# Lower halves of 18 of h's 49 tiles: by diagonal matmuls on TensorE and a copy on ScalarE instead of one instruction on VectorE

## The chip, the cores and the metric

The kernel runs on one core of a Trainium2 chip, as one launch. The metric is the device time of that launch in microseconds. Before the change it was 1441.87 us, the median of three runs (1438.64 to 1441.97).

## The reference, cut to what matters

A layer of a graph network: 6250 nodes with 256 values each, 200,000 edges sorted by target, a mixture of 64 experts with the best two for each node, a batch norm, and a layer norm at the end. What bears on the change is its first part:

```python
deg_out = jnp.clip(segment_sum(ones, src, num_segments=n), 1.0)
h = feats * jax.lax.rsqrt(deg_out)[:, None]
m = segment_sum(h[src], dst, num_segments=n) * jax.lax.rsqrt(deg_in)[:, None]
gc = m @ W_gc + b_gc
x = gc + (feats @ W_res + b_res)
```

The kernel multiplies by W_gc first, so its rows of h are feats @ W_gc times the factor rsqrt(deg_out) of their node, which it calls s_out.

## The kernel before, in words

The nodes are held in 49 tiles of 128 rows (NS = 49, the last tile with 106). A first stage, up to about 155 us, finds the degrees by matmuls of one-hots and projects the nodes (`project`). What it projects lands unscaled in `hrow[:, u, D:2D]`, by a DMA from the tile `hx` (line 623).

Then each row is scaled and split in two numbers, so that TensorE's faster float32r format keeps its accuracy: `upper(t)` (line 404, ScalarE) writes the product with s_out, rounded to float32r, into `hrow[:, u, :D]`, and `lower(t)` (line 409, VectorE) puts what the rounding left, product minus upper half, in the place of the unscaled values. Both work on two tiles a call, t - 1 and t, with t odd; `halves(t)` calls the two. After every four or six tiles `lower` writes these rows to `h_dram` (line 192, on SyncE's queue).

The stage that uses h is `dense()`. It is a generator of pieces of work; the loop at line 1176 runs them in the order in which they are yielded, and puts in pieces of another kind (`gather`) by their estimated durations. Inside `tc.manual_schedule()` each engine's instructions stand in this written order, and each engine works through its own in order; only semaphores tie them together. `dense()` runs windows c of edges:

- `lo_of` and `hot_of` (lines 386 and 837, VectorE) make tables of one-hots, `count(g)` (line 859, TensorE) multiplies two of them into a bank `pc` of PSUM, ScalarE casts the bank to `room` (line 871, 876 or 879), and VectorE adds its first column (line 902, `carried`).
- `multiply(c, t)` (lines 914 and 915, TensorE) multiplies the counts of window c by the lower and the upper half of tile t. The counts of window c + 1 are made between the multiplies of window c.
- In the opening (40 counts of window 0) a call of `halves` follows each four counts, which make one bank. From there, as long as tiles are left, one follows every second multiply of window 0, with about three counts between two calls.

The rows of h that went to DRAM come back in `gather`: GpSimd fetches 128 of them at a time by index (line 768), TensorE multiplies them (lines 773 and 774). The first fetch waits until all of h is written. The stage of the experts and the norms begins at about 880 us and isn't touched.

PSUM is cut into pools. The pool `ps_g` has one bank, in which `gather` adds up, as the tile `pg`.

Of the kernel before, what the change touches and what calls it, by code (L numbers as in the profile page):

```python
# [9 lines left out]
F32 = mybir.dt.float32  # L10
F32R = mybir.dt.float32r
# [4 lines left out]
AF = mybir.ActivationFunctionType  # L16
# [13 lines left out]
NS = -(-N // SP)  # L30
ODD = N - (NS - 1) * SP
D = 256
# [8 lines left out]
WIN = 128  # L41
# [8 lines left out]
FIRSTS = 32  # L50
PAIRS = 8
MARGIN = 48


SIZES = ((1, 416), (2, 400), (3, 368), (5, 352), (7, 320), (10, 288), (12, 272), (17, 256), (21, 240), (25, 224), (31, 208), (34, 192), (40, 176), (45, 160), (46, 144), (50, 128), (63, 112), (64, 80))
# [119 lines left out]
def gnn_moe_kernel(ctx, tc, x_in, x_cols, src, dst, bases, nexts, firsts, parts, lasts, W_gc, b_gc, W_res, b_res, Wg, bg, w1, b1, w2, b2,  # L175
                   gamma, beta, out):
    nc = tc.nc
    V, S, G, T = nc.vector, nc.scalar, nc.gpsimd, nc.tensor
# [9 lines left out]
    def source_out(tile_ap, ap, t0, n):  # L188

        whole = min(n, NS - 1 - t0)  # L190
        if whole > 0:
            nc.sync.dma_start(out=ap[t0 * SP:(t0 + whole) * SP, :].rearrange("(t p) d -> p t d", p=SP),
                              in_=tile_ap[:, :whole, :])
        if t0 + n >= NS:
            for a, b in ((0, 96), (96, ODD)):
                nc.sync.dma_start(out=ap[(NS - 1) * SP + a:(NS - 1) * SP + b, :], in_=tile_ap[a:b, NS - 1 - t0, :])
# [24 lines left out]
    def f32(ap):  # L221
        return ap.bitcast(F32)
# [128 lines left out]
    with tc.tile_pool(name="edges", bufs=1) as ep, ExitStack() as later:  # L351
# [50 lines left out]
        def upper(t):  # L402
            for u in range(t - 1, min(t + 1, NS)):
                S.activation(hrow[:, u, :D], f32(hrow[:, u, D:2 * D]), AF.Copy, scale=s_out[:, u:u + 1])

        def lower(t):
            at = range(t - 1, min(t + 1, NS))
            for u in at:
                V.scalar_tensor_tensor(hrow[:, u, D:2 * D], f32(hrow[:, u, D:2 * D]), s_out[:, u:u + 1],
                                       f32(hrow[:, u, :D]), op0=ALU.mult, op1=ALU.subtract)  # L410
            if t % 5 == 4 or t % 10 == 5:
                n = 6 if t % 10 == 5 else 4
                n -= max(t + 1 - NS, 0)
                t0 = at[-1] + 1 - n
                source_out(f32(hrow[:, t0:t0 + n, :2 * D]), h_dram, t0, n)

        def halves(t):
            upper(t)
            lower(t)

        with tc.tile_pool(name="late", bufs=1) as lp, tc.tile_pool(name="both", bufs=2) as bp, \
                tc.tile_pool(name="deg", bufs=1) as dp, tc.tile_pool(name="hot", bufs=2) as hp, \
# [325 lines left out]
        with tc.tile_pool(name="xs", bufs=1) as xs, tc.tile_pool(name="hotg", bufs=2) as hg, \  # L748
# [6 lines left out]
            for i in range(2):  # L755
                for t0 in range(0, NS, 10):
                    G.memset(f32(counts[i][:, t0:min(t0 + 10, NS), :]), 0.0)

            NR = 8
            ring = []  # L760
            for i in range(NR):
# [382 lines left out]
            def gather(n):  # L1144
                i, g = rows[n]
                g0, k = GATHER[i]
                if g == g0:
                    live["pg"] = ps_g.tile([WIN, D + 2], F32, name="pg")
                hot, further = batch.pop(n)
                if further is not None:  # L1150
                    hot_rows(further)
                top = i == len(GATHER) - 1
                add_rows(live["pg"], ring[n % NR], hot, g == g0, top and g == g0 + k - 1)
                if n + NR < len(rows):
                    fetch(ring[n % NR], srcg[:, rows[n + NR][1] - GD:rows[n + NR][1] - GD + 1])
                if g == g0 and not top:
                    live["overg"] = rows_of(ND + i + 1, "overg")
                if g == g0 + k - 1:
                    if not top:
                        T.matmul(live["pg"], live["overg"], ends_met["gather"], start=False, stop=True)  # L1160
                    res = rsp.tile([WIN, D + 2], F32, name="resg")
                    S.copy(res, live["pg"])
                    sums_done(res, ND + i)
                    ends_met["gather"] = res
                    made["gathered"] = i
# [828 lines left out]
    with tc.tile_pool(name="fin", bufs=1) as fp, tc.tile_pool(name="gat", bufs=4) as gp, \  # L1994
# [46 lines left out]
        t0 = 0  # L2041
# [139 lines left out]
```

## Time and profile before

| | us |
|---|---|
| median of three runs | 1441.87 |
| the profiled execution, its own time | 1442.04 |
| its span, first to last instruction | 1440.4 |
| TensorE busy | 1334.3 (93%) |
| VectorE busy | 1079.3 (75%) |
| ScalarE busy | 803.4 (56%) |
| mean granted clock of TensorE | 0.971 |

A share of the whole span is a mean over stages with different limits. The change lies between 155 and 200 us, so the rows below are from there, with a few from elsewhere for the durations of operations. In the rows PE is TensorE, DVE VectorE, ACT ScalarE, POOL GpSimd, SPq the queue of SyncE; "L409" is line 409. A row with "x4" stands for four instructions, from the first start to the last end. Brackets name how long the engine was idle before, and who ended that.

### The profile page before, as it was taken

The numbers are of one execution on the slowest core, as the hardware profiler recorded it, in microseconds if no ns is written. First come the engines' busy times: TensorE is split into PE (matmuls) and PEld (weight loads), VectorE is DVE, ScalarE is ACT, GpSimd is POOL, SyncE is SP. The second block draws the span as 40 slices with busy tenths as digits, with TensorE's granted clock in tenths as the row PEclk, the third lists the DMA queues.
The fourth block names the chain that finished last, engine by engine and source line by source line (L and its number), as shares of the span: only waits on it lengthen the run. The fifth ranks groups of instructions, "written<-read, shape, count | busy, mean of one in ns | idle before, by whom it ended". The sixth has DMA issues, their size and how long they took to land. (4 is left out here: it accounts for less than half of the span.)

```text
span 1440.4 us, 32497 instructions
## 1 busy us (share of the span) xinstructions
PE 1334.3 (93%) x9814; PEld 1121.1 (78%) x9814; DVE 1079.3 (75%) x3326; ACT 803.4 (56%) x2127; POOL 758.1 (53%) x894
## 2 busy tenths in 40 slices
PE   8999578999999999999999998799999999999683
PEld 4555367888889999999999996688788998799441
DVE  9999889999989888777777768655555555544588
ACT  7898646577776666656555532533333333333358
POOL 6000337777667776766777643255465556565100
PEclk9999699999999999999999999899999999999897
DMA  6667676777778787788778764789788888687645
GB/s 213 192 206 221 223 244 180 208 227 217 206 223 228 211 234 221 216 227 228 218 214 229 208 189 137 170 237 300 258 274 280 257 253 261 212 266 237 248 142 168
DMA packets 198010, 319.89 MB, mean 222 GB/s; under 512 B 27345, under 2 KB 129595, under 8 KB 197826
## 3 DMA queue, kind: packets, MB, share of 16 engines
q1 hardware_dynamic: 149716, 170.68, 38.2%
q0 software_dynamic: 47888, 146.88, 35.4%
q8 instruction: 79, 1.29, 0.4%
q14 instruction: 105, 0.86, 0.2%
q10 hardware_dynamic: 222, 0.19, 0.0%
HBM read 250.84 MB, written 60.35 MB: 216 GB/s over the span
## 5 line engine op out<-in xcount | busy, mean ns | idle before, releaser
L768 POOL DMA_INDIRECT r<-h_dram,srcg x445 | 470.5, 1057 | 215.9 <-PE pc L859 70.6
L914 PE MATMUL sm<-hrow,room 128*128 128x258 f32 x1470 | 486.8, 346 | 5.2 <-DVE room L902 5.0
L879 ACT CAST room<-pc 128x196 f32 (+7 forms) x879 | 356.5, 406 | 163.2 <-PE pc L859 125.2
L915 PE MATMUL sm<-hrow,room 128*128 128x256 f32 x1470 | 394.7, 282 | 0.0
L859 PE MATMUL pc<-hotk,lo 128*128 128x245 bf16 (+7 forms) x1118 | 302.6, 303 | 24.0 <-DVE lo L386 12.9
L837 DVE TENSOR_TENSOR hotk<-key,iota_h 128x784 bf16<-128x784 f16 (+4 forms) x488 | 247.8, 508 | 96.1 <-PE pc L859 91.3
L914 PEld LDWEIGHTS sm<-hrow,room 128*128 128x128 f32 x1470 | 287.5, 196 | 12.4 <-issue 7.3
L915 PEld LDWEIGHTS sm<-hrow,room 128*128 128x128 f32 x1470 | 279.7, 190 | 1.2
L1674 ACT ACTIVATE hT<-ph,bc 128x112 f32<-128x112 f32 (+16 forms) x256 | 108.3, 427 | 257.9 <-PE ph L1672 252.7
L902 DVE TENSOR_TENSOR room<-pc,room 128x49 f32 x908 | 197.5, 240 | 12.5 <-ACT room L879 5.5
L1672 PE MATMUL ph<-xgT,w1s 128*128 128x112 f32 (+17 forms) x1024 | 201.5, 341 | 0.5 <-DVE xgT L1655 0.4
L1630 POOL DMA_INDIRECT y_dram<-ys,dest x124 | 120.0, 968 | 138.9 <-ACT ys L1726 100.1
L1672 PEld LDWEIGHTS ph<-xgT,w1s 128*128 128x128 f32 x1024 | 166.8, 193 | 20.1 <-issue 2.3
L1630 POOL DMA_INDIRECT xg<-x_dram,ids x124 | 120.4, 971 | 62.5 <-DMA w1s<-in_L_gnn_w_dram 21.4
L859 PEld LDWEIGHTS <-lo 128*128 128x128 bf16 x1118 | 97.9, 100 | 62.6 <-DVE lo L386 14.3
L773 PE MATMUL pg<-r,hot 128*128 128x258 f32 x445 | 143.2, 322 | 3.5 <-DMA r<-h_dram,srcg 1.8
L774 PE MATMUL pg<-r,hot 128*128 128x256 f32 x445 | 125.2, 281 | 0.0
L1688 PE MATMUL py<-w2s,hT 128*128 128x256 f32 (+3 forms) x424 | 103.0, 386 | 0.9 <-DVE y_sum L1727 0.9
L1655 DVE TENSOR_SCALAR xgT<-pte,bsum 128x112 f32<-128x112 f32 (+14 forms) x128 | 48.7, 422 | 70.2 <-PE pte L1652 69.8
L611 PE MATMUL pr<-room,f 128*128 128x512 f32 x196 | 99.6, 633 | 0.0
L1710 PE MATMUL ph<-hT,w2s 128*128 128x208 f32 (+9 forms) x480 | 98.1, 358 | 0.0
L386 DVE TENSOR_TENSOR lo<-lo_b,iota 128x1024 bf16<-128x1024 bf16 x140 | 95.9, 685 | 0.0
(374 smaller groups left out, 1942.6 us busy)
## 6 DMA issues: line engine op xcount, KB each, us to landing
w1s<-in_L_gnn_w_dram SPq DMA_DIRECT2D x64, 512.0 KB
w2s<-in_L_gnn_w_dram SPq DMA_DIRECT2D x64, 512.0 KB
yr<-y_dram SPq DMA_DIRECT2D x10, 1024.0 KB
h_dram<-hrow SPq DMA_DIRECT2D x5, 1536.0 KB
r<-h_dram,srcg POOLq DMA_INDIRECT x445
f<-in_x_cols_dram SPq DMA_DIRECT2D x25, 256.0 KB
z_dram<-zeros SPq DMA_DIRECT2D x7, 903.0 KB
r_dram<-hx SPq DMA_DIRECT2D x24, 256.0 KB
```

The lines of the kernel that those rows point to most:

```text
L768: G.indirect_dma_start(out=f32(r[:, :2 * D]), out_offset=None, in_=h_dram[:, :], in_offset=bass.IndirectOffsetOnAxis(ap=idx, axis=0))
L773: T.matmul(pg, hot, r[:, D:], start=first, stop=False)
L774: T.matmul(pg[:, :D], hot, r[:, :D], start=False, stop=last)
L837: V.tensor_tensor(hot, pairs(key, e, n, m), iota_h[:, None, :m, :].to_broadcast([128, n // 2, m, 2]), ALU.is_equal)
L859: T.matmul(pc, los[g // PAIRS][:, r // 2, :, r % 2], hots.pop(g), start=(i == 0), stop=(i == k - 1))
L879: put = S.copy(counts[c % 2][:, :, 1:][:, :, ds(at, w - 1)], pc[:, :, 1:])
L902: add = V.tensor_tensor(to, more, f32(had), ALU.add).ins
L914: T.matmul(sm, by, hrow[:, t, D:], start=(t == 0), stop=False)
L915: T.matmul(sm[:, :D], by, hrow[:, t, :D], start=False, stop=(t == NS - 1))
L1630: w = G.indirect_dma_start(**kw)
L1672: T.matmul(ph[:, :m], w1s[:, kk, c * 128:(c + 1) * 128], xgT[:, kk, :m], start=(kk == 0), stop=(kk == 1))
L1674: S.activation(hT[:, c, :m], ph[:, :m], AF.Gelu, bias=b1_e[:, c:c + 1])
```

## The change

For the odd tiles from 5 to 39 (`TURNED`, 18 of them), `lower` no longer issues VectorE's instruction. ScalarE makes a table `scales`, a 128x128 matrix with s_out on its diagonal, by scaling the identity. At the next call of `halves`, `by_products` has TensorE multiply the unscaled rows by it (float32) and add the upper half times minus the identity (`less`, float32r) in the same half of a PSUM bank; at the call after that, ScalarE copies the bank's half to the lower half's place in `hrow`. So two calls lie between a tile's table and its copy. The bank's two halves are used in turn. The bank is a tile of the pool `ps_g`, whose one bank `gather` uses later. A write of rows to DRAM is issued once every tile in it has been copied (`rows_to_dram`).

```diff
--- before.py
+++ after.py
@@ -50,6 +50,7 @@
 FIRSTS = 32
 PAIRS = 8
 MARGIN = 48
+TURNED = range(5, 40, 2)
 
 
 SIZES = ((1, 416), (2, 400), (3, 368), (5, 352), (7, 320), (10, 288), (12, 272), (17, 256), (21, 240), (25, 224), (31, 208), (34, 192), (40, 176), (45, 160), (46, 144), (50, 128), (63, 112), (64, 80))
@@ -403,20 +404,46 @@
             for u in range(t - 1, min(t + 1, NS)):
                 S.activation(hrow[:, u, :D], f32(hrow[:, u, D:2 * D]), AF.Copy, scale=s_out[:, u:u + 1])
 
+        ahead, outs, low = [], [], {}
+
+        def by_products():
+            for u, done in list(ahead):
+                at = low["bank"][:, u // 2 % 2 * D:u // 2 % 2 * D + D]
+                if done:
+                    S.activation(hrow[:, u, D:2 * D], at, AF.Copy)
+                    ahead.remove((u, done))
+                else:
+                    T.matmul(at, low.pop(u), f32(hrow[:, u, D:2 * D]), start=True, stop=False)
+                    T.matmul(at, low["less"], hrow[:, u, :D], start=False, stop=True)
+                    ahead[ahead.index((u, done))] = (u, True)
+
+        def rows_to_dram():
+            while outs and all(u >= sum(outs[0]) for u, done in ahead):
+                t0, n = outs.pop(0)
+                source_out(f32(hrow[:, t0:t0 + n, :2 * D]), h_dram, t0, n)
+
         def lower(t):
             at = range(t - 1, min(t + 1, NS))
             for u in at:
+                if u in TURNED:
+                    low[u] = low["pool"].tile([128, 128], F32, name="scales", bufs=2)
+                    S.activation(low[u], ident, AF.Copy, scale=s_out[:, u:u + 1])
+                    ahead.append((u, False))
+                    continue
                 V.scalar_tensor_tensor(hrow[:, u, D:2 * D], f32(hrow[:, u, D:2 * D]), s_out[:, u:u + 1],
                                        f32(hrow[:, u, :D]), op0=ALU.mult, op1=ALU.subtract)
             if t % 5 == 4 or t % 10 == 5:
                 n = 6 if t % 10 == 5 else 4
                 n -= max(t + 1 - NS, 0)
                 t0 = at[-1] + 1 - n
-                source_out(f32(hrow[:, t0:t0 + n, :2 * D]), h_dram, t0, n)
+                outs.append((t0, n))
+            rows_to_dram()
 
         def halves(t):
+            by_products()
             upper(t)
             lower(t)
+            assert t < NS - 1 or not ahead
 
         with tc.tile_pool(name="late", bufs=1) as lp, tc.tile_pool(name="both", bufs=2) as bp, \
                 tc.tile_pool(name="deg", bufs=1) as dp, tc.tile_pool(name="hot", bufs=2) as hp, \
@@ -756,6 +783,10 @@
                 for t0 in range(0, NS, 10):
                     G.memset(f32(counts[i][:, t0:min(t0 + 10, NS), :]), 0.0)
 
+            low["pool"] = xs
+            low["bank"] = ps_g.tile([128, 2 * D], F32, name="pg")
+            low["less"] = xs.tile([128, 128], F32R, name="less")
+            S.activation(low["less"], ident, AF.Copy, scale=-1.0)
             NR = 8
             ring = []
             for i in range(NR):
@@ -1145,7 +1176,7 @@
                 i, g = rows[n]
                 g0, k = GATHER[i]
                 if g == g0:
-                    live["pg"] = ps_g.tile([WIN, D + 2], F32, name="pg")
+                    live["pg"] = ps_g.tile([WIN, 2 * D], F32, name="pg")[:, :D + 2]
                 hot, further = batch.pop(n)
                 if further is not None:
                     hot_rows(further)
```

How the instructions stand. First ScalarE at the start of the stretch, before the change: `hx` is the last projection, `room` takes the counts, line 404 makes the upper halves.

```order
L618 COPY hx_2741<-pr_2738 128x512 [waits DMAHW7_49,DMAHW6_49,PE_49]
L404 ACTIVATE hrow_110<-hrow_110,s_out_109 128x256 x4
L847 TENSOR_LOAD places_105 [waits DVE_49]
L871 CAST room0_2777<-pc_2838 128x49x2 [waits PE_49,DMASW2_49,Activation_49,Pool_49]
L404 ACTIVATE hrow_110<-hrow_110,s_out_109 128x256 x2
L879 ISA
L879 COPY room0_2777<-pc_2869 128x49 [waits PE_49,Activation_49]
L404 ACTIVATE hrow_110<-hrow_110,s_out_109 128x256 x2
L879 ISA
L879 COPY room0_2777<-pc_2881 128x49 [waits PE_49,Activation_49]
```

After the change, from the same place on: line 789 makes `less`, 430 a table `scales`, 413 is the copy out of the bank `pg`, 405 the upper halves, 902 and 910 the casts of counts.

```order
L645 COPY hx_2741<-pr_2738 128x512 [waits DMAHW7_49,DMAHW6_49,PE_49]
L789 ACTIVATE less_2790<-ident_66 128x128 [waits DMAHW3_49,DMAHW2_49,DMAHW4_49,DMAHW1_49,DMAHW5_49,DMAHW0_49,Activation_49]
L405 ACTIVATE hrow_110<-hrow_110,s_out_109 128x256 x2
L430 ACTIVATE scales_2833<-ident_66,s_out_109 128x128
L405 ACTIVATE hrow_110<-hrow_110,s_out_109 128x256 x2
L430 ACTIVATE scales_2842<-ident_66,s_out_109 128x128
L878 TENSOR_LOAD places_105 [waits DVE_49]
L902 CAST room0_2777<-pc_2844 128x49x2 [waits DMASW2_49,PE_49,Pool_49]
L413 ACTIVATE hrow_110<-pg_2789 128x256 [waits Activation_49]
L405 ACTIVATE hrow_110<-hrow_110,s_out_109 128x256 x2
L430 ACTIVATE scales_2876<-ident_66,s_out_109 128x128 [waits Activation_49]
L910 ISA
```

`less` has come between the last projection and the upper halves, with a wait for DMAs, and each cast of counts is followed by a copy of line 413, two upper halves and a table.

TensorE at the same place, before: the last projections, and counts (line 859), of which four make a bank `pc`; one pair of rows of four is shown for each of the first two banks.

```order
L611 MATMUL pr_2738<-room1_141,f_2415 128x512 [waits DMAHW5_49]
L611 MATMUL pr_2738<-room1_141,f_2415 128x512
L859 LDWEIGHTS lo_2815 [waits DMASW0_49,DVE_49,DMASW4_49,PE_49,Activation_49]
L859 MATMUL pc_2838<-hotk_2817,lo_2815 128x98 [waits Activation_49]
L859 LDWEIGHTS lo_2815
L859 MATMUL pc_2869<-hotk_2817,lo_2815 128x98
```

After: lines 416 and 417 are the two new matmuls; of each group of four counts one pair of rows or one row is shown.

```order
L416 MATMUL pg_2789<-hrow_110,scales_2833 128x256 [waits DMAHW4_49,DMAHW3_49,DMAHW5_49,DMAHW2_49,DMAHW6_49,DMAHW1_49,DMAHW7_49,DMAHW0_49,Activation_49]
L417 MATMUL pg_2789<-hrow_110,less_2790 128x256
L890 LDWEIGHTS lo_2818 [waits DMASW0_49,DMASW4_49,DVE_49,PE_49]
L890 MATMUL pc_2844<-hotk_2820,lo_2818 128x98 [waits PE_49]
L416 MATMUL pg_2789<-hrow_110,scales_2842 128x256 [waits Activation_49]
L417 MATMUL pg_2789<-hrow_110,less_2790 128x256
L890 MATMUL pc_2879<-hotk_2820,lo_2818 128x98
L416 MATMUL pg_2789<-hrow_110,scales_2876 128x256 [waits Activation_49]
L417 MATMUL pg_2789<-hrow_110,less_2790 128x256
```

In front of each group of four counts stand the two new matmuls, and the first of them waits for ScalarE each time.

TensorE somewhat later, when the multiplies of window 0 run (lines 914 and 915), before; of the three counts of a round one is shown.

```order
L914 MATMUL sm0_2813<-hrow_110,room0_2777 128x258
L915 MATMUL sm0_2813<-hrow_110,room0_2777 128x256
L914 MATMUL sm0_2813<-hrow_110,room0_2777 128x258
L915 MATMUL sm0_2813<-hrow_110,room0_2777 128x256
L859 LDWEIGHTS lo_3035
L859 MATMUL pc_3073<-hotk_2927,lo_3035 128x147 [waits PE_49]
L914 MATMUL sm0_2813<-hrow_110,room0_2777 128x258
L915 MATMUL sm0_2813<-hrow_110,room0_2777 128x256
```

After (lines 945 and 946 are the multiplies, 890 the counts, of which one of three is shown), up to the next new matmul:

```order
L416 MATMUL pg_2789<-hrow_110,scales_3125 128x256 [waits Activation_49]
L417 MATMUL pg_2789<-hrow_110,less_2790 128x256
L945 MATMUL sm0_2816<-hrow_110,room0_2777 128x258
L946 MATMUL sm0_2816<-hrow_110,room0_2777 128x256
L945 MATMUL sm0_2816<-hrow_110,room0_2777 128x258
L946 MATMUL sm0_2816<-hrow_110,room0_2777 128x256
L890 LDWEIGHTS lo_3085
L890 MATMUL pc_3154<-hotk_3006,lo_3085 128x147 [waits PE_49]
L416 MATMUL pg_2789<-hrow_110,scales_3148 128x256 [waits Activation_49]
```

The four multiplies and three counts of a round are as before; the two new matmuls, with a wait for ScalarE, stand in front of them.

## Rows read from the trace of the kernel before

**Rows 1.** Engines' busy time, TensorE's granted clock and DMA, by stretch.
```profile
core 0: us, PE busy (x) PEld busy (x) DVE busy (x) ACT busy (x) POOL busy (x), PEclk, DMA share, GB/s
148.30:151.70 3.40, 2.61 (x34) 1.97 (x34) 1.72 (x5) 0.62 (x2) 1.02 (x1) 0.51 0.02 5
158.50:161.90 3.40, 0.31 (x7) 0.31 (x8) 3.40 (x9) 2.81 (x9) 3.40 (x4) 1.00 0.59 214
165.30:175.30 10.00, 1.67 (x16) 1.27 (x17) 9.90 (x28) 6.04 (x19) 0.00 (x0) 0.50 0.97 363
175.30:179.00 3.70, 3.69 (x19) 3.42 (x20) 3.50 (x9) 1.48 (x6) 0.00 (x0) 0.50 1.02 382
179.00:185.80 6.80, 5.52 (x48) 4.58 (x47) 6.50 (x19) 6.63 (x21) 0.00 (x0) 0.99 0.76 289
189.20:192.70 3.50, 2.34 (x14) 1.95 (x13) 3.50 (x11) 1.24 (x6) 0.00 (x0) 0.52 1.01 373
```

**Rows 2.** VectorE in order of time: start, us, engine, line, operation.
```profile
164.12 0.87 DVE L409 SCALAR_TENSOR_TENSOR hrow<-hrow,s_out 128x256 fp32r<-128x256 f32 x2
...
173.12 0.87 DVE L409 SCALAR_TENSOR_TENSOR hrow<-hrow,s_out 128x256 fp32r<-128x256 f32 x2
...
178.15 0.88 DVE L409 SCALAR_TENSOR_TENSOR hrow<-hrow,s_out 128x256 fp32r<-128x256 f32 x2
...
189.98 0.48 DVE L409 SCALAR_TENSOR_TENSOR hrow<-hrow,s_out 128x256 fp32r<-128x256 f32 x1
```

**Rows 3.** TensorE in order of time, before and in the stretch of the change.
```profile
150.54 2.08 PE L611 MATMUL pr<-room,f 128*128 128x512 f32 x2
...
161.59 0.56 PE L859 MATMUL pc<-hotk,lo 128*128 128x98 bf16 x8 [3.13 <-DVE lo L386]
164.25 0.84 PE L859 MATMUL pc<-hotk,lo 128*128 128x98 bf16 x8 [2.10 <-DVE lo L386]
...
175.31 0.55 PE L914 MATMUL sm<-hrow,room 128*128 128x258 f32 x1 [4.35 <-DVE room L902]
...
176.78 0.60 PE L859 MATMUL pc<-hotk,lo 128*128 128x147 bf16 x3
...
178.13 0.59 PE L859 MATMUL pc<-hotk,lo 128*128 128x147 bf16 x3
...
179.32 0.38 PE L859 MATMUL pc<-hotk,lo 128*128 128x147 bf16 x3
...
180.05 0.38 PE L859 MATMUL pc<-hotk,lo 128*128 128x147 bf16 x3
```

**Rows 4.** TensorE in a later stretch: float32 matmuls of 256 columns.
```profile
1001.90 1.96 PE L1688 MATMUL py<-w2s,hT 128*128 128x256 f32 x8
```

**Rows 5.** ScalarE in order of time, around line 404 and 879.
```profile
157.77 1.71 ACT L404 ACTIVATE hrow<-hrow,s_out 128x256 fp32r<-128x256 f32 x4
...
162.05 0.24 ACT L879 CAST room<-pc 128x49 f32 x1 [0.74 <-PE pc L859]
162.14 0.91 ACT L404 ACTIVATE hrow<-hrow,s_out 128x256 fp32r<-128x256 f32 x2
...
164.85 0.27 ACT L879 CAST room<-pc 128x49 f32 x1 [0.91 <-PE pc L859]
```

**Rows 6.** ScalarE, line 918: a copy of 258 columns out of PSUM.
```profile
L918 ACT ACTIVATE resd<-sm,okc x30: 458/476/479, 205.1 to 870.3; 128x258 f32<-128x258 f32 x30
```

**Rows 7.** The 16 DMA engines from 160 to 162 us, 0.05 us a digit.
```profile
DMA  9999721000006499897989979899897998979979
```

**Rows 8.** SyncE's queue: issue of the last load of h's rows, and the writes.
```profile
158.71 0.50 SPq L623 DMA_DIRECT2D hrow<-hx  x1
159.69 31.55 SPq L192 DMA_DIRECT2D h_dram<-hrow  x10
```

**Rows 9.** GpSimd's first fetch of h's rows, and what it waited for.
```profile
199.02 1.09 POOL L768 DMA_INDIRECT r<-h_dram,srcg  x1 [35.91 <-DMA h_dram<-hrow]
```

**Rows 10.** TensorE's first matmul on fetched rows.
```profile
209.32 0.36 PE L773 MATMUL pg<-r,hot 128*128 128x258 f32 x1
```

## The prediction

> **What bounds the kernel now.** I read the busy shares of the page first, then the stretch of the change cut into windows, then the engines' rows in it in order of time. The chain that ended last is of no use here, since it covers only the end of the program. From 158.5 to 175.3 us VectorE is busy without a break (3.40 of 3.40 us, then 9.90 of 10.00), while TensorE works 0.31 and 1.67 us and its granted clock falls to 0.50 [rows 1]. So VectorE's order sets the pace: TensorE waits 2 to 3 us for each table of one-hots [rows 3], and VectorE finishes a pair of tiles every 1.50 us in the opening ((173.12 - 164.12) / 6) and every 1.48 us in the next part ((189.98 - 178.15) / 8) [rows 2]. Two of its lower halves take 0.87 us, so one is worth about 0.40 us. That is the 18 x 0.40 = 7.2 us which the change can take off VectorE.
>
> **The change part by part.**
>
> Removed: 18 of VectorE's 49 lower halves, one of each pair, from tile 5 to tile 39. VectorE alone would then need 1.50 - 0.40 = 1.10 us a pair.
>
> Added on ScalarE, per pair: a 128x128 table of factors and a copy of 128x256 out of PSUM. A table lies below a 128x256 activation, of which four take 1.71 us [rows 5], so below 0.43, and above nothing; I take 0.30, since half of the columns go. The copy is priced by the 258-column activation out of PSUM, 0.48 [rows 6]. With the two upper halves (0.86) and the small cast of counts (0.09, from 162.05 to 162.14 [rows 5]) ScalarE has 0.86 + 0.30 + 0.40 + 0.09 = 1.65 us of work a pair (the copy's last 0.08 lie under its successor). That is already more than the 1.50 us that VectorE took.
>
> Added on TensorE, per tile: a float32 matmul of 256 columns and one in float32r. Eight float32 pieces of 256 columns, two to a matmul, take 1.96 us at the full clock [rows 4], so a matmul is about 0.45, and 0.9 at the half clock (two pieces of 512 columns take 2.08 at 0.50 [rows 3], which gives 1.04 with the tail). For the second I use the group of three counts and four multiplies: 1.35 us at half clock (176.78 to 178.13), 0.73 at full (179.32 to 180.05) [rows 3], so some 0.25 and 0.14 a multiply.
>
> Added waits. This is what decides. The four counts stand behind the two new matmuls on TensorE, ScalarE's cast stands behind the counts, the copy of the tile stands behind the cast, and the next tile's new matmul waits for that copy. So the three form one loop, which nothing lets run ahead:
> half clock: cast 0.09 + copy 0.48 + matmuls 0.9 + 0.25 + from the counts' start to the next cast 0.60 (164.25 to 164.85) [rows 3, 5] + about 0.13 for the hand-overs = 2.45 us;
> full clock: 0.09 + 0.48 + 0.45 + 0.14 + 0.46 (161.59 to 162.05) [rows 3, 5] + 0.08 = 1.7 us.
> Once the multiplies have begun, the group of three counts and four multiplies stands in the place of the four counts, with 0.27 (half) or 0.18 (full) from the last count's issue to the cast, as above: 0.09 + 0.48 + 0.9 + 0.25 + 1.35 + 0.27 + 0.06 = 3.4 us at half clock, 0.09 + 0.48 + 0.45 + 0.14 + 0.73 + 0.18 + 0.13 = 2.2 us at full. Behind the waiting cast and copy on ScalarE stand the next upper halves, for which VectorE's other lower halves wait; so VectorE falls to the loop's pace.
> The Trainium skill's page "PSUM — Partial Sum Buffer" (section Terms) calls it an error when TensorE writes and ScalarE reads one bank at once. The order agrees: the two halves of the one bank are used in turn, and yet the matmul for tile 7 waits for ScalarE, behind the copy of tile 5. With a bank for each, the copy would leave the loop, some 0.5 us in each of 18 rounds, and the sum would come to some 9 us less.
>
> A wait at the start. The table "less" lies where "hx" lay, and waits for the DMAs that read it; the last of them loads tile 48, is issued at 158.71 [rows 8] and is through at about 160.35, where the DMA engines go quiet [rows 7]. ScalarE before went on at 157.77 with the upper halves of tiles 4 to 7 [rows 5]. So it stands for 2.5 us, and VectorE behind it.
>
> The sum at half clock. "less" at about 160.4; it, two upper halves and a table: 0.2 + 0.86 + 0.4, so the first new matmul at 161.9. Ten loops to that of tile 25: 186.4. From there to tile 27's no counts lie between: 0.9 + 0.25 + 0.2 until its result is read + 0.48 + 0.07 = 1.9, then its own 1.15: the first multiply at 189.4 against 175.31 [rows 3], +14.1. Six loops from tile 27 to 39: 6 x 3.4 = 20.4 against 6 x 1.48 = 8.9, +11.5. After tile 39 the old order is back. TensorE's own pauses there, at half clock from 189.2 to 192.7 (2.34 of 3.50 busy [rows 1]), can give back 1 to 2 us, since VectorE is then no longer late. 14.1 + 11.5 - 1.6 = +24.
>
> At full clock: first multiply at 161.9 + 17.0 + 1.4 + 0.6 = 180.9, +5.6; 6 x 2.2 against 8.9, +4.3; together +9.9, less 1: +9.
>
> Which clock? It fell to its lower level (1.2 GHz, 0.50) after 158.5 to 161.9, in which TensorE worked 0.31 of 3.40 us [rows 1]. The new wait leaves TensorE idle in the same place, so I expect the same fall. It rose to the upper level (2.4 GHz) at 179.0, after TensorE had worked 3.69 of 3.70 us without a pause, and did not rise after 189.2 to 192.7 (2.34 of 3.50) or 148.3 to 151.7 (2.61 of 3.40) [rows 1]. The new loop has a pause of some 0.7 us in every round (copy, cast and hand-overs), so I take the lower level as long as the loop lasts. The Trainium skill's page "TensorE: Matmul & The Clock Gate" (Part 1) says that the throttled state is the default and that sustained activity releases it; the trace agrees, but no row shows a stretch with pauses like the loop's.
>
> The rest moves as a block. The writes of h and the first fetch (199.02) [rows 8, 9] come later with the lower halves, TensorE's first use of a fetched row (209.32) [rows 10] with the multiplies, by about the same amount. What follows on each engine is written out in order behind it. The first write of h, at 159.69 [rows 8], now waits for the copy of tile 5 (about 164.5); behind it in SyncE's queue stand only the other writes. The wider tile for the gathered sums is used through the same 258 columns and costs nothing; its bank is free after the copy of tile 39, some 15 us before the first fetched row is used. The profiled execution took 1442.04 us (span 1440.4 and 1.6 around it), 0.2 above the median of the runs, so sums on either stand the same: 1442 + 24 = 1466 us.
>
> **The rivals.**
> 1. The clock rises during the loop, or does not fall. For it: in the second part the pause of 0.7 us comes only once in 3.4 us, and 2.61 of 3.40 is the fullest stretch that is seen to fail [rows 1]. Full in the second part alone: 14.1 + 4.3 - 1 = +17, 1459 us; full throughout: +9, 1451 us.
> 2. Only ScalarE's work counts, the loop being shorter than I think (the matmuls go ahead of the copy, or the copy is nearer 0.3). Then 2.5 at the start and 18 x (1.65 - 1.50) = 2.7: +5, 1447 us. Against it: the order in which the copy stands behind the cast.
> 3. Faster: VectorE's 7.2 us come off the path. This needs a loop below 1.49 us, so a TensorE that takes the new matmuls without adding to the 0.46 us from counts to cast. It gives -7.2 + 2.5 = -4.7, 1437 us. For it: TensorE is idle for most of 158.5 to 175.3 [rows 1]. Against it: the loop's parts are added up in a row, not side by side.
> 4. No change: the writes of h fill the DMA engines (shares of 0.97 and 1.02 from 165.3 to 179 [rows 1], ten issued within 31.55 us [rows 8]), so an earlier or slightly later VectorE leaves the end of the writes alone. Against it: TensorE uses the first fetched row 10.3 us after the first fetch begins (199.02 to 209.32), so the writes are not what it waits for.
>
> **How the numbers follow.** A measurement of this kernel can tell about 0.3% from no change, 4.3 us. Half clock throughout, 1466: 0.50. The clock high in a part or throughout, 1451 to 1459: 0.30. ScalarE alone, 1447: 0.07, of which half lies within 0.3%. No change: 0.06. Faster: 0.07, of which 0.01 lies within 0.3%. So faster 0.06, same 0.10, slower 0.84. The range 1447 to 1473 leaves out the last two cases and a little above; the upper end is the half-clock case with 1.04 instead of 0.9 for the float32 matmul in 18 tiles (+2.5), nothing given back (+1.6) and 0.1 more a loop (+1.8). The half-clock case alone reaches from 1458 to 1473.
>
> **What would show it.** Right: new float32 matmuls 2.4 us apart at granted clock 0.50 up to about 186 us, then 3.4 apart; the first multiply near 189; "less" begins near 160.4 with ScalarE idle before it; VectorE idle in front of line 433, waiting for the upper halves; the first fetch near 223. Wrong: VectorE still without a pause in 160 to 190, new matmuls under 1.5 us apart, or ScalarE's copy beginning before the counts behind it have ended.

## The result, and the profile after

The changed kernel takes 1463.27 us (median of 6 runs, 1459.21 to 1467.05), the kernel before, beside it, 1441.61 (6 runs, 1438.64 to 1444.58). The ratio is 1.0156, 95% interval 1.0142 to 1.0170: 21.7 us slower, where +24 was forecast. The profiled execution is the fastest of the six: 1459.21 us, span 1457.6. Beside the later experiments (from "The second part alone" on) the kernel before itself takes 1528 us, for a reason that no run shows, so each experiment is given by its ratio to the kernel before that ran beside it.

First, the point from which the two traces are compared. ScalarE's root of the degrees, which lies ahead of all that the change touches, begins at 153.62 us before,
```profile
153.62 0.24 ACT L736 ACTIVATE s_out<-s_out 128x49 f32<-128x49 f32 x1 [4.69 <-DVE s_out L735]
```
and at 155.10 in the changed kernel:
```profile
155.10 0.24 ACT L763 ACTIVATE s_out<-s_out 128x49 f32<-128x49 f32 x1 [4.69 <-DVE s_out L762]
```
In the later runs it lies between 153.2 and 154.6. So 1.48 us of the two profiles' difference is scatter; below, times "after the root" are used.

ScalarE of the changed kernel in order of time (answers to [rows 5]):
```profile
161.40 0.31 ACT L789 ACTIVATE less<-ident 128x128 fp32r<-128x128 f32 x1 [2.92 <-DMA hrow<-hx]
...
167.29 0.25 ACT L910 CAST room<-pc 128x49 f32 x1 [0.85 <-PE pc L890]
167.38 0.39 ACT L413 ACTIVATE hrow<-pg 128x256 fp32r<-128x256 f32 x1
```
The wait of "less" for the DMAs is there, 2.92 us. So is the order of the loop: the cast waits for the counts, the copy (L413) stands behind the cast. TensorE, opening and second part (answers to [rows 3]):
```profile
162.96 1.22 PE L416 MATMUL pg<-hrow,scales 128*128 128x256 f32 x2 [5.45 <-ACT scales L430]
...
165.41 1.22 PE L416 MATMUL pg<-hrow,scales 128*128 128x256 f32 x2 [0.66 <-ACT hrow L413]
166.07 0.78 PE L417 MATMUL pg<-hrow,less 128*128 128x256 f32 x1
166.64 0.55 PE L890 MATMUL pc<-hotk,lo 128*128 128x98 bf16 x4
167.82 1.22 PE L416 MATMUL pg<-hrow,scales 128*128 128x256 f32 x2 [0.63 <-ACT hrow L413]
...
187.17 1.22 PE L416 MATMUL pg<-hrow,scales 128*128 128x256 f32 x2 [0.63 <-ACT hrow L413]
...
190.37 0.42 PE L945 MATMUL sm<-hrow,room 128*128 128x258 f32 x1
...
192.99 0.70 PE L416 MATMUL pg<-hrow,scales 128*128 128x256 f32 x2 [0.67 <-ACT hrow L413]
...
202.23 0.70 PE L416 MATMUL pg<-hrow,scales 128*128 128x256 f32 x2 [1.17 <-ACT hrow L413]
...
204.41 0.70 PE L416 MATMUL pg<-hrow,scales 128*128 128x256 f32 x2 [0.67 <-ACT hrow L413]
```
Ten rounds from 162.96 to 187.17 are 2.42 us each, and every new matmul waits 0.63 or 0.66 us for the copy of the tile before. In the second part the same matmul takes 0.70 in place of 1.22 us, and five rounds from 192.99 to 204.41 are 2.28 us each (four of 2.2, one of 2.68). The windows show why (answers to [rows 1]):
```profile
core 0: us, PE busy (x) PEld busy (x) DVE busy (x) ACT busy (x) POOL busy (x), PEclk, DMA share, GB/s
165.30:175.30 10.00, 7.37 (x29) 4.92 (x30) 4.64 (x10) 6.59 (x22) 0.00 (x0) 0.50 0.70 262
175.30:189.10 13.80, 10.15 (x38) 6.50 (x38) 7.04 (x18) 9.03 (x30) 0.00 (x0) 0.50 0.50 190
189.10:192.50 3.40, 3.17 (x13) 2.50 (x13) 1.24 (x3) 1.41 (x5) 0.00 (x0) 0.53 0.73 283
192.50:206.00 13.50, 9.14 (x62) 7.55 (x63) 7.23 (x19) 9.38 (x29) 0.00 (x0) 1.00 0.55 206
```
The granted clock is 0.50 (1.2 GHz) through the opening and 1.00 (2.4 GHz) from 192.5 to 206, after TensorE had worked 3.17 of 3.40 us. VectorE, busy 9.90 of 10 us before, is busy 4.64 of 10: it was relieved, and it waits. Who waits for whom, 155 to 225 us (us in total, times, longest):
```profile
ACT room L910 <- PE pc L890: 18.4, 24, 2.0
DVE hrow L433 <- ACT hrow L405: 18.0, 18, 2.8
PE pg L416 <- ACT hrow L413: 11.4, 17, 1.2
```
The first and the third line are the loop: ScalarE waits for the counts, TensorE for the copy. The second is VectorE, which waits for the upper halves behind both. What follows came later as a block (answers to [rows 6, 8, 9, 10]): the writes of h, the first fetch, the first fetched row on TensorE, and the ends of the 30 windows.
```profile
165.38 45.87 SPq L193 DMA_DIRECT2D h_dram<-hrow  x10
218.72 1.31 POOL L799 DMA_INDIRECT r<-h_dram,srcg  x1 [55.07 <-DMA h_dram<-hrow]
229.10 0.36 PE L804 MATMUL pg<-r,hot 128*128 128x258 f32 x1
L949 ACT ACTIVATE resd<-sm,okc x30: 461/477/479, 225.1 to 890.8; 128x258 f32<-128x258 f32 x30
```
The first window ends 20.0 us later than before (225.1 against 205.1), the last 20.5 later (890.8 against 870.3). The rest of the span is 566.8 us here and 570.1 before. In four later profiles of variants (the first four experiments) it is 570.1 to 571.9; with those this execution would have taken 1462.5 to 1464.3 us, like the median.

### The profile page after: what moved, and what is told of

It is laid out like the page before. It is cut to its first block, busy times and chain, and to the rows that moved or that the text cites. A ratio compares the mean times of both kernels' runs of the same rounds, so it can differ in the third digit from the quotient of the medians.

```text
span 1457.6 us, 32626 instructions
## 1 busy us (share of the span) xinstructions
PE 1351.2 (93%) x9868; PEld 1131.5 (78%) x9868; DVE 1075.3 (74%) x3308; ACT 816.1 (56%) x2164; POOL 754.9 (52%) x894
## 3 DMA queue, kind: packets, MB, share of 16 engines
q0 software_dynamic: 47888, 146.88, 35.3%
## 5 line engine op out<-in xcount | busy, mean ns | idle before, releaser
L890 PE MATMUL pc<-hotk,lo 128*128 128x245 bf16 (+7 forms) x1118 | 303.5, 304 | 11.5 <-DVE room L933 8.8
```

Source lines behind the costliest of these rows:

```text
L890: T.matmul(pc, los[g // PAIRS][:, r // 2, :, r % 2], hots.pop(g), start=(i == 0), stop=(i == k - 1))
```

## The experiments

The first four ran beside a kernel before that takes 1443.0 us. In their profiles the last of the 30 windows ends 726 to 738 us after the root. In those of the later experiments it ends 762 to 780 us after it, for example (two banks and early tables, the second time):
```profile
L951 ACT ACTIVATE resd<-sm,okc x30: 459/476/482, 209.7 to 923.3; 128x258 f32<-128x258 f32 x30
```
From 400 to 500 us TensorE is busy 98.8 to 99.0% of the time in the first four and 93.6 to 95.3% in the later ones. So some 40 of the 85 us lie ahead of the last window's end (769 us here, 726 with two banks alone), in a stretch that no edit touches, and there is no profile of the kernel before beside the later ones. Stretches are therefore compared after the root, and only up to the first fetched rows. (The expectation of that run puts all the slowness behind 880 us, which holds for about half of it, and a wait of 6.9 us down to fetched rows, where the profile names only "remote".)

**Two PSUM banks.**
```diff
-  at = low["bank"][:, u // 2 % 2 * D:u // 2 % 2 * D + D]
+  at = low["banks"][u // 2 % 2][:, :D]
...
+  low["banks"] = [spare_bank, banks[1]]      # the bank of pg, and one of the sums
```


> The changed kernel, but the results of two neighbouring turned tiles go to two PSUM banks in place of two halves of one (the second bank is that of the odd windows' sums, which is not in use yet). Theory (a loop through the one bank: cast, copy, next tile's new matmul, counts, cast): the copy leaves the loop, since the next tile's matmul no longer waits for it. TensorE has 1.24 us of new matmuls and 0.57 of counts a round at the half clock, ScalarE about 1.65 (0.86 + 0.29 + 0.39 + 0.09), so a round of the opening falls from 2.42 to 1.65 to 1.8 us (10 rounds: 6 to 8 us) and one of the second part from 2.2 to 1.65 (6 rounds: 3 us). New matmuls 1.65 to 1.8 us apart, first multiply near 183.5 us, time 1452 to 1454 us. Rival (ScalarE's work with its hand-overs sets the pace, whatever the bank): rounds of 2.4 us and 1463 us as before this edit.

1450.3 us, ratio 1.0045 (1.003 to 1.006). TensorE's new matmuls at the start and in the opening:
```profile
165.35 1.22 PE L416 MATMUL pg<-hrow,scales 128*128 128x256 f32 x2 [0.19 <-ACT scales L430]
166.92 0.66 PE L416 MATMUL sm<-hrow,scales 128*128 128x256 f32 x2
...
170.25 0.70 PE L416 MATMUL sm<-hrow,scales 128*128 128x256 f32 x2 [0.44 <-ACT scales L430]
171.71 0.70 PE L416 MATMUL pg<-hrow,scales 128*128 128x256 f32 x2 [0.44 <-ACT scales L430]
```
No new matmul waits for a copy any more; they wait for ScalarE's tables. With the pauses gone the clock rises in the opening, and a round takes 1.45 us, less than the 1.65 expected: from start to start ScalarE's cast takes 0.08 us, the copy 0.27, two upper halves 0.80 and the table 0.29, less than their durations. ScalarE is now the bound:
```profile
165.30:175.30 10.00, 7.28 (x46) 5.13 (x47) 7.51 (x18) 9.65 (x35) 0.00 (x0) 0.92 0.93 347
```
9.65 of 10 us busy. The loop through the one bank is shown, and it, with the clock that it kept low, is the larger part of the loss.

**Tables early, in places of their own.**
```diff
+  less = ep.tile([128, 128], F32R, name="less")
...
+  S.activation(less, ident, AF.Copy, scale=-1.0)      # near 150 us
...
+  low["pool"] = ep                                    # the tables of factors
```


> The changed kernel, but the table of -1 (less) is made earlier, where ScalarE waits anyway (near 150 us), and it and the two tables of factors lie in places of their own, not where hx lay. Theory: the wait of 2.9 us for the DMAs that read hx goes, and everything behind it comes earlier by that: first new matmul near 160.0 us, first multiply near 187.4, time 1460 to 1461 us. The rounds themselves stay at 2.42 and 2.2 us. Rival (the writes of h, or VectorE's tables of one-hots, would make ScalarE or TensorE wait as long in the same place): first multiply where it was, 1463 us.

1459.45 us, ratio 1.0118 (1.0092 to 1.0145): about 5 us less than the change by the ratios. The first new matmul comes 4.49 us after the root (157.92 - 153.43) in place of 7.86, the first multiply 31.2 in place of 35.3. But the first window's end is not earlier (69.8 after the root against 70.0), since here the clock falls in the second part:
```profile
193.85 0.70 PE L417 MATMUL pg<-hrow,scales 128*128 128x256 f32 x2 [0.68 <-ACT hrow L414]
196.53 1.03 PE L417 MATMUL pg<-hrow,scales 128*128 128x256 f32 x2 [1.16 <-ACT hrow L414]
199.70 1.22 PE L417 MATMUL pg<-hrow,scales 128*128 128x256 f32 x2 [0.67 <-ACT hrow L414]
```
So the wait at the start costs 3.4 us up to the first new matmul and 4.0 up to the first multiply, a little more than the 2.9 expected. And the second part's clock may go either way: with the same instructions it stayed at 1.00 in the changed kernel's profile and fell to 0.50 in this one.

**The copy ahead of the cast, one bank.**
```diff
   if i == 0:
+      copies()            # the copies out of PSUM, at the window's first count
       live["pc"] = ps_c.tile([128, 512], F32, name="pc")
```


> The changed kernel with one bank, but ScalarE copies a tile out of PSUM ahead of its cast of the counts that follow it, not behind. Theory of the loop: the counts and the cast leave the loop; what is left of it at the half clock is new matmuls 1.24, hand-over, copy 0.4 to 0.5, which is 1.8 to 1.9 us and lies beside ScalarE's 1.65. TensorE has 1.81 us of work a round. So the opening's rounds fall from 2.42 to about 1.85 us (10 rounds: 5.7 us), the second part's from 2.2 to 1.65 or 1.7 (6 rounds: 3 us): time 1453 to 1456 us. Rival (ScalarE's work with its hand-overs sets the pace): rounds of 2.4 us, 1463 us. Were it the collision of a writing TensorE and a reading ScalarE in one bank that costs, this would stay above the kernel with two banks by the copy's time in each of 16 rounds, 6 us or more.

1457.6 us, ratio 1.01 (1.008 to 1.0119), less gain than expected. At the half clock rounds are 1.97 us (167.95, 169.92, 171.89), near the 1.85; once the clock is up, some take 3 us:
```profile
173.86 0.70 PE L421 MATMUL pg<-hrow,scales 128*128 128x256 f32 x2 [0.18 <-ACT hrow L413]
...
175.39 0.70 PE L421 MATMUL pg<-hrow,scales 128*128 128x256 f32 x2 [0.52 <-ACT hrow L413]
...
178.36 0.70 PE L421 MATMUL pg<-hrow,scales 128*128 128x256 f32 x2 [1.95 <-ACT hrow L413]
...
182.86 1.22 PE L421 MATMUL pg<-hrow,scales 128*128 128x256 f32 x2 [1.88 <-ACT hrow L413]
```
In the rounds that end at 178.36 and 182.86 ScalarE's load of eight places from SBUF into registers stands ahead of the cast:
```profile
L883 ACTq TENSOR_LOAD <-places x1: 1753/1753/1753, 174.8 to 174.8; - x1
```
It takes 1.75 us, and the cast begins when it has ended (176.74); the same at 179.3, with the cast at 181.24. The DMA engines are full at both (shares 1.02 and 0.98). In the changed kernel's opening these two loads take 0.55 and 0.80 us (at 177.1 and 181.9), lie in ScalarE's wait for the counts and cost nothing; a third, at 201.2, stands ahead of the copy whose round takes 2.68 us. The order of copy and cast was part of the loop, but this cure uncovered another wait.

**The pause filled.**
```diff
+  for _ in range(8):      # in the opening, ahead of the matmuls that wait for the copy
+      T.matmul(low["fill"][:, 128:226], lo_b[:, :128], lo_b[:, :98], start=True, stop=True)
```


> The changed kernel, but TensorE fills its pause in each round of the opening with eight matmuls of 98 columns (bf16) that nobody reads, into a bank that is not in use yet, ahead of the new matmuls that wait for the copy. Theory: the opening is at the half clock because of that pause, and what the half clock costs is the difference of 2.42 to about 1.7 us a round. If the granted clock then rises to 2.4 GHz in the opening, the fill takes 0.55 us of a pause of about 0.65 and a round takes 1.7 us: 10 rounds, 7 us less, or 1456 us (less of it the later it rises). If it stays at 1.2 GHz, the fill takes 1.1 us in place of a pause of 0.63, a round takes 2.9 us and the kernel is slower by 4 to 5 us, 1468 us.

1457.1 us, ratio 1.0093 (1.0075 to 1.0111).
```profile
167.00 1.22 PE L422 MATMUL pg<-hrow,scales 128*128 128x256 f32 x2
...
169.36 0.70 PE L422 MATMUL pg<-hrow,scales 128*128 128x256 f32 x2 [0.28 <-ACT hrow L419]
171.00 0.70 PE L422 MATMUL pg<-hrow,scales 128*128 128x256 f32 x2 [0.28 <-ACT hrow L419]
```
Matmuls that nobody reads make the kernel 6 us faster than the change (1463.3 to 1457.1; 9 by the ratios): the clock rises near 169 us and a round takes 1.65 us (1.7 expected). The half clock in the opening was the work of the pause, and cost what the sum said.

**The second part alone.** TURNED = range(27, 40, 2).

> The changed kernel with only tiles 27, 29, ... 39 turned (the second part, in which the multiplies run); the opening keeps VectorE's lower halves. What the second part costs by itself, and which clock it has when the opening before it is not the loop. Theory: the wait of 2.9 us at the start stays (ScalarE has the table of -1 to make either way, and VectorE is behind it), the opening keeps its 1.50 us a pair, and the six rounds take 2.2 us in place of 1.48 at 2.4 GHz, 3.4 at 1.2 GHz: 2.9 + 4.3 + 1 (the last two copies before the first multiply) = +8, 1450 us at the upper clock, 2.9 + 11.5 + 1 = +15, 1457 to 1458 us at the lower. The opening's part is then the rest of the +21: 11 to 13 us without the wait. Rival (all the loss lies in the opening, and the second part's rounds hide behind the counts and the writes): +3 us, 1445 us.

Ratio 1.0127 (1.0103 to 1.0152), +18 us on 1442, 3 more than the lower clock's case.
```profile
184.30 1.22 PE L416 MATMUL pg<-hrow,scales 128*128 128x256 f32 x2 [0.67 <-ACT hrow L413]
187.68 1.22 PE L416 MATMUL pg<-hrow,scales 128*128 128x256 f32 x2 [0.69 <-ACT hrow L413]
...
194.60:198.60 4.00, 3.02 (x11) 2.45 (x12) 0.89 (x3) 2.25 (x8) 0.00 (x0) 0.50 0.71 270
```
Here the second part runs at 0.50 throughout, with 3.37 us in four of its five full rounds (3.85 in the other): the forecast's 3.4 to 0.03. TensorE was busy 3.02 of 4.00 us, and the clock did not rise. In the changed kernel, whose second part began after 3.17 of 3.40 us of work, it did.

**Two banks and early tables**, twice.

> The changed kernel with both edits: two PSUM banks, and the tables made and placed where nothing waits for the DMAs that read hx. If the loop and the wait add up, 1450.3 - 2.9 to 3.9 = 1446 to 1447.5 us, with new matmuls 1.45 us apart in the opening (ScalarE's work a round) and 1.8 in the second part. What is left over the kernel before (some 4 us) is then ScalarE, which has 1.45 us of work a round and no slack: its rounds of the second part, 1.8 against 1.48. Rival: TensorE starts at 2.4 GHz here and stays there, since it has no idle time of 5 us before it, and the opening is faster from its first round: 1444 us.

> The kernel with two PSUM banks and early tables once more, beside a kernel before that takes 1443 us: the first time both were some 6% slower behind 880 us of the run, and waited up to 6.9 us for fetched rows at 205 to 213 us, which hides what is asked here. Theory: the first multiply is 0.4 us later than before, so the opening costs nothing any more; the second part still has 1.8 us a round in place of 1.48: 2 to 3 us slower than before, 1445 us. Rival (loss and gain in the second part do not reach the end, since the first fetch comes at the same time as before): 1442 to 1443 us, no difference.

Ratios 1.0059 (1.0034 to 1.0084) and 1.0051 (1.0024 to 1.0078), not below the kernel with two banks alone. The first multiply is 22.1 and 22.7 us after the root, against 21.69 before: the opening costs only 0.4 to 1.0 us any more, with the clock up in most of its rounds. The second part's rounds of 1.8 us take some of it back, and from 209 us on comes a stretch in which all engines wait:
```profile
209.40:213.40 4.00, 0.48 (x5) 0.44 (x5) 1.15 (x4) 1.65 (x5) 0.95 (x1) 1.00 0.71 215
```
TensorE works 0.48 of 4.00 us. Like stretches stand in most other profiles of the later experiments and in neither the kernel before nor the one with two banks alone; their cause is not settled, and with it how much of the 0.5% is due to the change.

**Nine tiles** (5, 9, ... 37), two banks, early tables.

> Two banks, early tables, and only every second of the turned tiles (5, 9, 13, ... 37: nine). ScalarE's work is then 1.45 and 0.95 us in turn, 1.2 on the mean, VectorE's 1.10 and 1.50, 1.3 on the mean: if VectorE and ScalarE set the pace and the two buffers of one-hots even it out, a pair takes 1.3 us in place of 1.50: 16 x 0.2 = 3.2 us less than the kernel before, 1440 us. Rival (no evening out: each round takes the longer of the two, 1.45 or 1.50): 1443 us, as before; if something behind the first multiply gives the time back, the same.

Ratio 1.0039 (1.0017 to 1.0061). Both were wrong. There is less work between the pauses, and TensorE's clock stays at 0.50 to 178 us,
```profile
166.10:170.10 4.00, 2.62 (x19) 1.99 (x18) 3.32 (x9) 2.46 (x8) 0.00 (x0) 0.50 1.00 372
```
and a pair takes 1.75 us (new matmuls at 164.89, 168.39 and 171.88, one in two pairs), where with all 18 it takes 1.45 once the clock is up. That the clock is the reason is likely and not shown, since TensorE, VectorE and ScalarE all have pauses there. The first multiply comes 22.8 us after the root, about as late as with all 18, and the kernel is not slower than that one.

**The opening alone** (tiles 5 to 25), two banks, early tables.

> Two banks, early tables, and only tiles 5 to 25 turned (the opening). ScalarE's 1.45 us a round against VectorE's 1.50 before, and the second part as in the kernel before. Theory: first multiply 0.4 us later than before, first window's end the same or up to 0.5 later: 1442 to 1443 us, no difference. Rival (the last copies of the opening hold up the second part): 1445 us or more.

Ratio 1.0039 (1.0008 to 1.007). The first window ends 51.3 us after the root, before 51.46, and the first fetch comes 45.0 after it, before 45.4. Up to there it equals the kernel before. TensorE's first fetched row comes 58.0 us after the root, before 55.7, behind one of those stretches in which all engines wait (TensorE is busy 0.59 of 2.00 us from 209 to 211); what of the 0.1 to 0.7% that the times show is due to the change stays open.

**What free help is worth.** Two kernels without the 18 lower halves, from the kernel before: in the first they are simply missing, in the second GpSimd sets them to zero.

> The kernel before without the lower halves of the 18 turned tiles: nothing takes their place, and those halves of h keep the unscaled values (this part of the computation is left out). It measures what the 18 x 0.40 = 7.2 us on VectorE are worth when the help costs nothing. Theory (VectorE's order sets the pace from 158 to 192 us of the kernel before): a pair of tiles takes 1.10 us on VectorE in place of 1.50, ScalarE 0.95; first multiply 4 to 4.5 us earlier, 1434 to 1437 us. Rival (the writes of h and the order behind them set the end, or another wait takes its place at once): first multiply earlier, but 1440 to 1443 us. If it is so, no way of moving these halves can gain.

> The kernel before, but the lower halves of the 18 turned tiles are set to zero by GpSimd, which is idle from 163 to 199 us, and not computed (this part of the computation, the small remainder of h that the upper half does not hold, is left out; unlike unscaled values it leaves the rest of the kernel its usual data). It measures the most that taking these halves off VectorE can give. With the halves simply missing, the first multiply came 3.5 us earlier, counted from the root of the degrees, and the first window's end 3.8 us earlier. Theory (the gain lies in the opening alone, where VectorE's order sets the pace; the second part has other limits): 3.5 to 4 us less than the kernel before, 0.25%. Rival (my forecast's 7.2 us): 0.5%. Rival (given back by the writes of h and the fetches): nothing.

With unscaled values a later part goes another way (13,023 us), so only the stretch up to its first fetched rows is read: first multiply 18.2 us after the root (3.5 earlier than before), first window's end 47.7 (3.8 earlier). The first fetch moves less, 2.2 us (196.64 - 153.41 against 199.02 - 153.62):
```profile
196.64 1.09 POOL L770 DMA_INDIRECT r<-h_dram,srcg  x1 [33.77 <-DMA h_dram<-hrow]
209.25 0.36 PE L775 MATMUL pg<-r,hot 128*128 128x258 f32 x1
...
162.00:175.00 13.00, 6.08 (x42) 4.98 (x43) 11.20 (x30) 8.71 (x28) 0.87 (x17) 0.50 1.03 377
180.00:185.00 5.00, 1.99 (x16) 1.36 (x15) 4.66 (x13) 4.51 (x16) 0.00 (x0) 1.00 1.03 379
```
The writes of h now fill the DMA engines without a break (before, their share was 0.68 from 180 to 185 us), and the first fetch waits for them. TensorE's first fetched row (209.25) comes no earlier at all, 55.8 us after the root against 55.7, behind a stretch from 207 to 209 us in which TensorE is busy 0.06 of 2.00; whether that stretch belongs to the change is not known. The zeros give a ratio of 1.0016 (0.9991 to 1.0041): no gain, with the first multiply 4.7 us earlier. They begin late, at 162.9, and hold up the first write (163.27), so this second run alone would prove little.

**GpSimd in the place of TensorE and ScalarE**, tiles 5 to 25.
```diff
...
+  G.tensor_scalar(scaled, f32(hrow[:, u, D:2 * D]), s_out[:, u:u + 1], None, op0=ALU.mult)
+  G.tensor_tensor(hrow[:, u, D:2 * D], scaled, f32(hrow[:, u, :D]), ALU.subtract)
```


> The kernel before, but GpSimd computes the lower halves of tiles 5, 7, ... 25 (h times the factor into a tile of its own, then minus the upper half): neither TensorE nor ScalarE nor PSUM takes part. A pair of tiles then takes VectorE 1.10 us in place of 1.50. If the two GpSimd instructions take together less than about 1.2 us a tile and do not slow VectorE, the first multiply comes 3.5 us earlier, 1438 to 1440 us. If they take 1.5 us or more a tile, GpSimd sets the pace of the opening and delays the writes of h: at 2 us a tile 11 x 0.5 = 5 us later, 1447 us. If VectorE and GpSimd hold each other up, VectorE's instructions grow longer in 163 to 185 us, and the gain is gone even at a short time a tile.

Ratio 1.0085 (1.0055 to 1.0114).
```profile
167.75 1.49 POOL L412 TENSOR_SCALAR scaled<-hrow,s_out 128x256 f32<-128x256 f32 x1
169.32 0.91 POOL L413 TENSOR_TENSOR hrow<-scaled,hrow 128x256 fp32r<-128x256 f32 x1
...
171.88 1.12 DVE L386 TENSOR_TENSOR lo<-lo_b,iota 128x1024 bf16<-128x1024 bf16 x1
...
L415 DVE SCALAR_TENSOR_TENSOR hrow<-hrow,s_out x16: 472/694/855, 173.5 to 187.4; 128x256 fp32r<-128x256 f32 x16
```
GpSimd takes 2.0 to 2.9 us a tile. Beside it some of VectorE's instructions are longer: one of eight tables of one-hots takes 1.12 in place of 0.68 us, and the lower halves that VectorE still makes take 0.47 to 0.86 (median 0.69 from 173 us on), where the 49 of the kernel before take 0.47 to 0.49. The first multiply is 4.5 us earlier, but the rows of h are ready late, the ten writes of h are issued up to 199.2 us (191.2 before), the DMA engines are full from 190 to 208 us, and the first fetch comes at 210.40. The profile puts the last of that wait down to another transfer (z_dram, issued at 206.97), so how much of it the writes of h cause is not settled. The loss, some 12 us by the ratio, is more than the 5 expected at 2 us a tile.

## Why the prediction was right, and where its size was off

- The wait of "less": 2.9 us against 2.5; the first new matmul 7.86 us after the root, 8.3 forecast.
- The loop: 2.42 us a round against 2.45. That the sum is right to 0.03 us is partly luck, since its parts are off and cancel: from 165.41 to 167.82 the float32 matmul takes 0.66 us from start to start, not 0.9, the second new matmul 0.57, not 0.25, the way from the copy's start to the next matmul 0.44, not 0.61, the counts to the cast 0.65, not 0.60. That they stand in a row is shown: without the bank in common the matmul no longer waits for the copy, and with the copy ahead of the cast the round at 0.50 falls to 1.97 us.
- The opening's sum: the first multiply 13.6 us later after the root (35.27 against 21.69), +14.1 forecast.
- The step that failed is "I take the lower level as long as the loop lasts". In the profiled execution the second part ran at 2.4 GHz, as the first rival had it, and added 18.5 - 13.6 = 4.9 us up to the first window's end in place of 11.5 - 1.6 = 9.9 (3.3 by the rival). The price at 1.2 GHz was right (3.37 us in the run with the last seven). What was not foreseen is the stretch between the two parts, 189.1 to 192.5, where the new matmuls of tile 27, the multiplies and the counts follow one another with hardly a pause (3.17 of 3.40 us). Of the six executions of the changed kernel the three above the median have a mean granted clock of 0.957 to 0.962, the three below it 0.966 to 0.970. So the longer ones may have had the lower level in the second part, as the run with early tables had; where in them the clock was low is not shown.
- So the sum by what was measured is 1.5 (ahead of the root) + 13.6 + 4.9 + 0.5 (to 890 us) = +20.5. The 1.5 is scatter, so the change itself accounts for 19.0 of the median's 21.7; the other 2.7 are not traced. The median lies between the forecast's main case (1466) and its first rival (1459), and the range holds both, so the time alone does not decide between them. That the profiled execution took the rival's 1459 is chance: its rest behind the last window was 3.3 us shorter than that of the kernel before.
- "With a bank for each" was put at 9 us less; the ratios give 16. The sum for it kept the lower clock, and the clock rose as well.
- The rival "faster": VectorE did lose 18 instructions, 7.2 us by the forecast's 0.40 each, but with free help only 3.5 us reach the first multiply, 3.8 the first window's end, 2.2 the first fetch and none TensorE's first fetched row. The writes of h are the next limit of the fetch, 2 us away, which the forecast's argument against its fourth rival overlooked. No variant beat the kernel before.

## What to carry to other kernels

Work that is given to idle engines must not tie them into a loop with the engine that it relieves: write down which instruction each of the new ones waits for, across all queues, and add the loop up before counting what the busy engine saves. Ask how far the next limit is, since it cuts off what is won beyond it (here the DMA engines left 2 of 3.5 us to the first fetch). And price TensorE's work at the clock of the stretch where it lands, which the pauses of the new work itself help to decide.

## What the runs showed of the hardware

- Useless matmuls can pay: eight a round (98 columns) brought the granted clock from 0.50 to 1.00 and the round from 2.42 to 1.65 us.
- Less work can take longer in a stretch: with nine turned tiles in place of 18 the clock stayed at 0.50 to 178 us, with 1.75 us a pair against 1.45. The kernel as a whole was not slower for it (ratios 1.0039, and 1.0051 and 1.0059).
- A load of eight values into ScalarE's registers took 0.54 to 0.76 us where the DMA engines were idle (shares 0.00 to 0.07), 0.80 and 0.81 at shares of 0.77 and 0.73, and 1.74 to 1.94 where they were full (0.98 to 1.02, four loads in two kernels).
- GpSimd's two instructions on 128x256 took 2.0 to 2.9 us a tile, and beside them VectorE's lower halves 0.47 to 0.86 us, where the kernel before has 0.47 to 0.49.
